# A graph-attention kernel in float32: the next group's q/k/v projections cut into quarters and laid between the attention steps of each batch

## The chip, the cores and the metric

The kernel runs on one core of a Trainium2 chip. The metric is the device time of one execution in microseconds (us), as the median of several runs. Before the change it was 3089.8 us (3 runs, 3089.11 to 3089.93). A program on one core shows no second core to compare with, so a run is called fast when it lies within 1.5% of the fastest run of the same kernel.

## The reference

The input is x of 128 batches, each 128 tokens by 512 features, with one 128x128 adjacency matrix adj. All of it is float32.

```python
# layer 0: edge convolution (both weights are adj), residual, layer norm
A = einsum('od,bdn->bon', adj, x);  C = A + b
x = layernorm(x + max over m of relu(A[m] + (C - A)[n]))
# layer 1: masked attention with 8 heads of 64, projection, layer norm, residual, layer norm
q, k, v = split(x @ w_qkv)
attn = softmax(where(adj == 0, -inf, q @ k.T * scale))
o = (attn @ v) @ w_proj + b_proj
x = layernorm(x + o + layernorm(o) * gamma + beta)
```

The largest products are the q/k/v projection (128x512 by 512x1536 for each batch) and the output projection (128x512 by 512x512). The batches do not depend on each other, which is what makes it possible to work on the projections of later batches while an earlier one is in its attention.

## The kernel before

Batches go in groups of four. `prepare(g)` does layer 0 of a group (`pa`, the normalisation, the transposes `ptx`) and then all projections of the group: eight chunks of q and k (`pq`, four matmuls each, over the 512 tokens of the group) and four of v (`pv`).

```python
def prepare(g):
    ...                                    # pa, layer norm, ptx -> xT
    for c in range(2 * KC):                # q and k: 8 chunks
        pq = ps_1.tile(...)
        for kc in range(KC):
            nc.tensor.matmul(pq, wqkv_sb[:, kc, c*P:(c+1)*P], xT[:, kc], ...)
        ...                                # q copied by ScalarE, k by VectorE, into qkT
    for i in range(G):                     # v: one chunk for each batch
        ...                                # pv, 4 matmuls; copied by ScalarE
```

`softmax` of a batch makes the scores (`psc`, eight small matmuls of 64 rows, which the trace has as 16 records, two for each float32 matmul; a transpose is one record: `ppt` has 8 for 8), adds the mask, takes the maximum, the eight exponentials, and divides. `finish` is the dependent tail, in which every TensorE step needs a copy by another engine of what the step before it made:

```python
def finish(g, i, xt, v, e):
    ...   # ppt: 8 transposes of e (TensorE) -> eT (ScalarE copy)
    ...   # pav: 8 pairs of head and value (TensorE) -> oT (ScalarE copy)
    ...   # po: output projection (TensorE) -> o, layer norms, y (VectorE, GpSimd)
```

The loop places the projections of the next group as one whole in the middle of a group:

```python
for g in range(NG):
    xt, qkT, v = ready
    for i in range(G):
        e = softmax(g, i, qkT)
        if pending is not None:
            finish(*pending)
        pending = (g, i, xt, v, e)
        if i == 1 and g + 1 < NG:
            ready = prepare(g + 1)         # 64 pq and 32 pv records in one piece
        ...
```

## Time and profile before

| | before |
|---|---|
| time, median | 3089.8 us |
| span of the profiled run | 3087.5 us |
| TensorE busy | 2555.4 us (83%) |
| TensorE idle (span less busy) | 532.1 us |
| VectorE busy | 1443.9 us (47%) |
| mean granted TensorE clock (1 is full speed) | 0.893 |
| chain that ended last, on TensorE | 60% |

The chain that ended last is the work followed back from the last instruction, at each step to what released it. The table is read in pairs. Busy 83% beside a chain that is on TensorE for only 60% says that TensorE often waits for another engine that waits for TensorE (ppt alone waits 319.2 us for VectorE). Idle time and clock belong together as well, because some of the busy time is work done at a lower clock: from 1503.17 to 1509.89 us, behind two waits, the clock is 0.54 and po takes 6.72 us, where at a clock of 1.00 it takes 3.70. The lines themselves stand in the prediction.

### The profile page before, as it was taken

How to read it: one execution, taken by the hardware profiler on the slowest of the kernel's cores; microseconds unless marked ns; L12 is line 12 of the kernel's file. 1: busy time of each engine (PE TensorE's matmuls, PEld its weight loads, DVE VectorE, ACT ScalarE, POOL GpSimd, SP SyncE). 2: the span in 40 equal slices, each digit the busy share in tenths (PEclk: the TensorE clock that was granted, in tenths of full speed). 3: DMA queues.
4: the chain of work that ended last, by engine and by line, in shares of the span. 5: the costliest groups of instructions: out<-in, count | busy, mean ns of one | idle time of the engine just before them, and what ended most of it. 6: DMA issues, size and time to landing. Idle time of an engine off the chain costs nothing.

```text
span 3087.5 us, 27231 instructions
## 1 busy us (share of the span) xinstructions
PE 2555.4 (83%) x9985; PEld 1331.7 (43%) x9985; DVE 1443.9 (47%) x2755; ACT 827.3 (27%) x2689; POOL 383.3 (12%) x422
## 2 busy tenths in 40 slices
PE   7877898777988779887798877888778987779887
PEld 3444444444444444444444444444444444444443
DVE  2355533555334553345543355433555335553346
ACT  1233222232222322223322223222232222322222
POOL 0011110111011111111110011100111101110112
PEclk9898999888998889988898888989889998889988
DMA  2000000000000000000000000000000000000000
GB/s 106 4 28 28 28 8 21 28 28 28 21 7 28 28 28 24 7 24 28 28 24 7 24 28 28 24 8 24 28 28 28 9 20 28 28 28 21 7 14 24
DMA packets 38293, 73.89 MB, mean 24 GB/s; under 512 B 2832, under 2 KB 2960, under 8 KB 38160
## 3 DMA queue, kind: packets, MB, share of 16 engines
q1 hardware_dynamic: 35328, 67.12, 6.3%
q10 hardware_dynamic: 2832, 5.05, 0.5%
q8 instruction: 78, 1.28, 0.2%
q14 instruction: 55, 0.45, 0.0%
HBM read 38.60 MB, written 33.55 MB: 23 GB/s over the span
## 4 chain that ended last, share of the span: by engine, by line
PE 60%; DVE 22%; POOL 6%; ACT 5%; issue 5%; POOLq 0%; DVEq 0%; ACTq 0%
PE pq L147 28%; PE pv L160 14%; PE po L214 11%; PE ptx L139 4%; DVE st L112 3%; POOL rstd L107 3%; ACT e L184 3%; POOL res L220 3%; DVE nmax L181 2%; DVE o L225 2%; PE pav L205 2%; DVE o L218 2%; DVE r L122 2%; DVE o L228 2%; DVE xt L127 2%
## 5 line engine op out<-in xcount | busy, mean ns | idle before, releaser
L147 PE MATMUL pq<-xT,wqkv_sb 128*128 128x512 f32 x2048 | 888.5, 594 | 1.4 <-ACT xT L140 1.3
L214 PE MATMUL po<-wproj_sb,oT 128*128 128x512 f32 x1024 | 565.1, 702 | 49.9 <-ACT oT L210 45.9
L147 PEld LDWEIGHTS pq<-xT,wqkv_sb 128*128 128x128 f32 x2048 | 389.5, 191 | 479.5 <-issue 476.7
L184 ACT ACTIVATE e<-e,nmax 128x128 f32<-128x128 f32 x1024 | 396.7, 389 | 405.8 <-DVE nmax L181 253.4
L160 PE MATMUL pv<-wqkv_sb,xT 128*128 128x512 f32 x1024 | 444.7, 592 | 0.0
L197 PE MATMUL ppt<-ident,e 128*128 128x128 f32 x1024 | 165.0, 306 | 319.2 <-DVE e L190 319.2
L154 DVE COPY qkT<-pq 128x512 f32<-128x512 f32 x128 | 88.6, 692 | 706.4 <-PE pq L147 706.4
L220 POOL TENSOR_TENSOR res<-xt,o 128x512 f32<-128x512 f32 x128 | 167.3, 1307 | 1999.5 <-DVE o L218 1994.2
L218 DVE TENSOR_TENSOR o<-po,bproj_sb 128x512 f32<-128x512 f32 x128 | 88.0, 688 | 678.8 <-PE po L214 678.7
L214 PEld LDWEIGHTS po<-wproj_sb,oT 128*128 128x128 f32 x1024 | 217.7, 224 | 312.5 <-issue 235.4
L197 PEld LDWEIGHTS ppt<-ident,e 128*128 128x128 f32 x1024 | 139.6, 161 | 383.0 <-issue 381.9
L107 POOL TENSOR_TENSOR rstd<-ve,mhalf 128x1 f32<-128x1 f32 (+1 forms) x288 | 216.7, 756 | 700.5 <-DVE ve L105 695.4
L160 PEld LDWEIGHTS pv<-wqkv_sb,xT 128*128 128x128 f32 x1024 | 194.6, 190 | 244.9 <-issue 244.9
L164 ACT COPY v<-pv 128x512 f32<-128x512 f32 x128 | 75.0, 586 | 803.6 <-PE pv L160 803.6
L205 PE MATMUL pav<-eT,v 128*64 128x128 f32 x2048 | 143.6, 284 | 89.5 <-ACT eT L199 89.2
L184 ACT ACTIVATION_READ_ACCUMULATOR e<-e,nmax 128x1 f32 x1024 | 191.8, 187 | 0.0
L140 ACT COPY xT<-ptx 128x512 f32<-128x512 f32 x128 | 74.3, 581 | 404.3 <-PE ptx L139 404.3
L205 PEld LDWEIGHTS pav<-eT,v 128*64 128x64 f32 x2048 | 111.7, 139 | 148.7 <-ACT eT L199 102.5
L179 DVE TENSOR_TENSOR e<-psc,mask 128x1024 f32<-128x1024 f32 x128 | 154.7, 1209 | 14.1 <-PE psc L174 14.1
L174 PE MATMUL psc<-qkT 64*128 64x128 f32 x2048 | 158.8, 289 | 1.1 <-ACT eT L199 1.1
L190 DVE TENSOR_TENSOR e<-e,rsum 128x1024 f32<-128x1024 f32 x128 | 156.2, 1220 | 1.2
L181 DVE TENSOR_REDUCE nmax<-e 128x8 f32<-128x1024 f32 x128 | 155.1, 1211 | 0.1
(34 smaller groups left out, 1758.8 us busy)
## 6 DMA issues: line engine op xcount, KB each, us to landing
xt<-in_x_dram SPq DMA_DIRECT2D x32, 1024.0 KB, 5.4
out_dram<-y SPq DMA_DIRECT2D x128, 256.0 KB, 2.0
wqkv_sb<-in_L_gnn_w_qkv_dram ACTq DMA_DIRECT2D x3, 1024.0 KB, 15.2
wproj_sb<-in_L_gnn_w_proj_dram ACTq DMA_DIRECT2D x1, 1024.0 KB, 18.8
bproj_sb<-in_L_gnn_b_proj_dram ACTq DMA_DIRECT2D x1, 256.0 KB, 14.4
gamma_sb<-in_L_gnn_ln_gamma_dram ACTq DMA_DIRECT2D x1, 256.0 KB, 10.5
beta_sb<-in_L_gnn_ln_beta_dram ACTq DMA_DIRECT2D x1, 256.0 KB, 10.5
adj_sb<-in_adj_dram ACTq DMA_DIRECT2D x1, 64.0 KB, 3.0
```

The lines of the kernel that those rows point to most:

```text
L107: nc.gpsimd.tensor_tensor(r, ve, mhalf[:, :n], op=ALU.pow)
L147: nc.tensor.matmul(pq, wqkv_sb[:, kc, c * P : (c + 1) * P], xT[:, kc], start=(kc == 0), stop=(kc == KC - 1),)
L160: nc.tensor.matmul(pv, xT[:, kc, i, :], wqkv_sb[:, kc, 2 * D :], start=(kc == 0), stop=(kc == KC - 1),)
L174: nc.tensor.matmul(psc[:, s, hp, :], qkT[rs, hp, i, :], qkT[rs, KC + hp, i, :], start=True, stop=True,)
L179: nc.vector.tensor_tensor(e, psc.rearrange("p s a m -> p (s a) m"), mask_b, op=ALU.add)
L181: nc.vector.tensor_reduce(nmax, e, AX.X, ALU.max, negate=True)
L184: nc.scalar.activation(e[:, j, :], e[:, j, :], AF.Exp, bias=nmax[:, j : j + 1], accum_out=sums[:, j : j + 1],)
L190: nc.vector.tensor_tensor(e, e, rsum[:, :, None].to_broadcast([P, H, P]), op=ALU.mult)
L197: nc.tensor.transpose(ppt[:, j, :], e[:, j, :], ident)
L205: nc.tensor.matmul(pav[s * HD : (s + 1) * HD, hp, :], v[:, i, h * HD : (h + 1) * HD], eT[:, s * HP + hp, :], start=True, stop=True,)
L214: nc.tensor.matmul(po, oT[:, c, :], wproj_sb[:, c, :], start=(c == 0), stop=(c == KC - 1),)
L220: nc.gpsimd.tensor_tensor(res, xt[:, i, :], o, op=ALU.add)
```

## The change

The intent is that TensorE always has something to do that waits for nothing, in each place where the attention chain would make it wait. The kernel's steps become small functions, and a loop over single batches issues them in a fixed order: between the score matmuls and `pav` lies a chunk of q, between `pav` and `po` a chunk of k, and behind `po` a chunk of v, all of the group that is needed five steps later. Layer 0 runs 9 and 14 steps ahead.

```diff
-    xpool = ctx.enter_context(tc.tile_pool(name="xpool", bufs=3))
+    xpool = ctx.enter_context(tc.tile_pool(name="xpool", bufs=7))
 ...   (prepare, softmax and finish are cut into conv, transpose_x, qk, vproj,
 ...    scores, transpose_e, attend and project, with the same instructions)
-    for g in range(NG):
-        ...
+    A_DENSE, A_TRANS, A_CONV = 5, 9, 14
+    with tc.manual_schedule(engines={mybir.EngineType.PE}):
+        for s in range(-A_CONV, B):
+            here, nxt = 0 <= s, 0 <= s + 1 < B
+            u, t, w = s + A_DENSE, s + A_TRANS, s + A_CONV
+            dense = 0 <= u < B
+            if w % G == 0 and w // G + 1 < NG:
+                load_x(w // G + 1)
+            if here:
+                eT = transpose_e(s)              # ppt
+            if nxt:
+                scores(s + 1)                    # psc of the next batch
+            if dense:
+                qk(u // G, u % G)                # pq, a chunk of q
+            if here:
+                oT = attend(s, eT)               # pav
+            if dense:
+                qk(u // G, KC + u % G)           # pq, a chunk of k
+            if here:
+                project(s, oT)                   # po
+            if dense:
+                vproj(u // G, u % G)             # pv
+            if 0 <= t < B:
+                transpose_x(t)                   # ptx
+            if w < B:
+                conv(w)                          # pa
```

The number of matmuls is the same. The four more tiles of x hold the batches that are now in flight.

More of the change, by code (lines that the diff above doesn't have):

```diff
@@ L45, in tile_adj_resnorm_d2 @@
     G = 4
+    NG = B // G
     KC = D // P
@@ L57, in tile_adj_resnorm_d2 @@
     ps_2 = ctx.enter_context(tc.tile_pool(name="ps_2", bufs=2, space=bass.MemoryType.PSUM))
+    xs, rs, qkTs, vs, xTs, es, mv0s = {}, {}, {}, {}, {}, {}, {}
     def load_x(g):
@@ L61, in load_x @@
         nc.sync.dma_start(xt, x[g * G : (g + 1) * G].rearrange("b t d -> t b d"))
-        return xt
+        xs[g] = xt
     adj_sb = const.tile([P, P], FP, name="adj_sb")
@@ L68, in tile_adj_resnorm_d2 @@
     nc.scalar.dma_start(b0_sb, b0.rearrange("(p o) -> p o", o=1))
-    x_tiles = {0: load_x(0)}
+    load_x(0)
     wqkv_sb = const.tile([P, KC, 3 * D], FP, name="wqkv_sb")
@@ L113, in stats, with conv @@
         nc.vector.bn_aggr(mv, st)
-    def prepare(g):
-        xt = x_tiles.pop(g)
-        r = small.tile([P, G], FP, tag="r", name=f"r_{g}")
-        for i in range(G):
-            pa = ps_1.tile([P, D], FP, tag="ps1", name=f"pa_{g}_{i}")
-            nc.tensor.matmul(pa, adjT, xt[:, i, :], start=True, stop=True)
-            nc.vector.tensor_reduce(r[:, i : i + 1], pa, AX.X, ALU.max)
+    def conv(b):
+        g, i = divmod(b, G)
+        xt = xs[g]
+        if i == 0:
+            rs[g] = small.tile([P, G], FP, tag="r", name=f"r_{g}")
+        pa = ps_1.tile([P, D], FP, tag="ps1", name=f"pa_{b}")
+        nc.tensor.matmul(pa, adjT, xt[:, i, :], start=True, stop=True)
+        nc.vector.tensor_reduce(rs[g][:, i : i + 1], pa, AX.X, ALU.max)
+        if i < G - 1:
+            return
+        r = rs.pop(g)
@@ L123, in prepare @@
         nc.vector.tensor_scalar(r, r, b0_sb, 0.0, op0=ALU.add, op1=ALU.max)
         mv = small.tile([P, G, 2], FP, tag="mv0", name=f"mv0_{g}")
-        for i in range(G):
-            nc.vector.tensor_scalar(xt[:, i, :], xt[:, i, :], r[:, i : i + 1], None, op0=ALU.add)
-            stats(mv[:, i, :], xt[:, i, :], f"0_{g}_{i}")
-        rstd = rstd_of(mv, G, f"0_{g}")
-        xT = group.tile([P, KC, G, P], FP, tag="xT", name=f"xT_{g}")
-        for i in range(G):
-            nc.vector.tensor_scalar(
-                xt[:, i, :], xt[:, i, :], mv[:, i, 0:1], rstd[:, i : i + 1],
-                op0=ALU.subtract, op1=ALU.mult,
-            )
-            pt = ps_1.tile([P, KC, P], FP, tag="ps1", name=f"ptx_{g}_{i}")
-            for c in range(KC):
-                nc.tensor.transpose(pt[:, c, :], xt[:, i, c * P : (c + 1) * P], ident)
-            nc.scalar.copy(xT[:, :, i, :], pt)
@@ L143, in prepare @@
-        qkT = group.tile([P, 2 * KC, G, P], FP, tag="qkT", name=f"qkT_{g}")
-        for c in range(2 * KC):
-            pq = ps_1.tile([P, G, P], FP, tag="ps1", name=f"pq_{g}_{c}")
-            for kc in range(KC):
-                nc.tensor.matmul(
-                    pq, wqkv_sb[:, kc, c * P : (c + 1) * P], xT[:, kc],
-                    start=(kc == 0), stop=(kc == KC - 1),
-                )
-            if c < KC:
-                nc.scalar.activation(qkT[:, c], pq, AF.Copy, scale=scale)
-            else:
-                nc.vector.tensor_copy(qkT[:, c], pq)
@@ L156, in prepare @@
-        v = group.tile([P, G, D], FP, tag="v", name=f"v_{g}")
-        for i in range(G):
-            pv = ps_1.tile([P, D], FP, tag="ps1", name=f"pv_{g}_{i}")
-            for kc in range(KC):
-                nc.tensor.matmul(
-                    pv, xT[:, kc, i, :], wqkv_sb[:, kc, 2 * D :],
-                    start=(kc == 0), stop=(kc == KC - 1),
-                )
-            nc.scalar.copy(v[:, i, :], pv)
-        return xt, qkT, v
-    def softmax(g, i, qkT):
-        psc = ps_2.tile([P, 2, HP, P], FP, tag="ps2", name=f"psc_{g}_{i}")
+        for j in range(G):
+            nc.vector.tensor_scalar(xt[:, j, :], xt[:, j, :], r[:, j : j + 1], None, op0=ALU.add)
+            stats(mv[:, j, :], xt[:, j, :], f"0_{g}_{j}")
@@ new lines, in conv, with transpose_x @@
+        mv0s[g] = mv, rstd_of(mv, G, f"0_{g}")
+    def transpose_x(b):
+        g, i = divmod(b, G)
+        xt = xs[g]
+        mv, rstd = mv0s[g]
+        if i == 0:
+            xTs[g] = group.tile([P, KC, G, P], FP, tag="xT", name=f"xT_{g}")
+        nc.vector.tensor_scalar(
+            xt[:, i, :], xt[:, i, :], mv[:, i, 0:1], rstd[:, i : i + 1],
+            op0=ALU.subtract, op1=ALU.mult,
+        )
+        pt = ps_1.tile([P, KC, P], FP, tag="ps1", name=f"ptx_{b}")
+        for c in range(KC):
+            nc.tensor.transpose(pt[:, c, :], xt[:, i, c * P : (c + 1) * P], ident)
+        nc.scalar.copy(xTs[g][:, :, i, :], pt)
@@ new lines, in qk @@
+    def qk(g, c):
+        xT = xTs[g]
+        if c == 0:
+            qkTs[g] = group.tile([P, 2 * KC, G, P], FP, tag="qkT", name=f"qkT_{g}")
+        pq = ps_1.tile([P, G, P], FP, tag="ps1", name=f"pq_{g}_{c}")
+        for kc in range(KC):
+            nc.tensor.matmul(
+                pq, wqkv_sb[:, kc, c * P : (c + 1) * P], xT[:, kc],
+                start=(kc == 0), stop=(kc == KC - 1),
+            )
+        if c < KC:
+            nc.scalar.activation(qkTs[g][:, c], pq, AF.Copy, scale=scale)
+        else:
+            nc.vector.tensor_copy(qkTs[g][:, c], pq)
@@ new lines, in vproj, with scores @@
+    def vproj(g, i):
+        xT = xTs[g]
+        if i == 0:
+            vs[g] = group.tile([P, G, D], FP, tag="v", name=f"v_{g}")
+        pv = ps_1.tile([P, D], FP, tag="ps1", name=f"pv_{g}_{i}")
+        for kc in range(KC):
+            nc.tensor.matmul(
+                pv, xT[:, kc, i, :], wqkv_sb[:, kc, 2 * D :],
+                start=(kc == 0), stop=(kc == KC - 1),
+            )
+        nc.scalar.copy(vs[g][:, i, :], pv)
+    def scores(b):
+        g, i = divmod(b, G)
+        qkT = qkTs[g]
+        psc = ps_2.tile([P, 2, HP, P], FP, tag="ps2", name=f"psc_{b}")
@@ L171, in softmax @@
         for hp in range(HP):
             for s in range(2):
-                rs = slice(s * HD, (s + 1) * HD)
+                hs = slice(s * HD, (s + 1) * HD)
                 nc.tensor.matmul(
-                    psc[:, s, hp, :], qkT[rs, hp, i, :], qkT[rs, KC + hp, i, :],
+                    psc[:, s, hp, :], qkT[hs, hp, i, :], qkT[hs, KC + hp, i, :],
                     start=True, stop=True,
                 )
-        e = work.tile([P, H, P], FP, tag="e", name=f"e_{g}_{i}")
+        e = work.tile([P, H, P], FP, tag="e", name=f"e_{b}")
@@ L179, in softmax @@
         nc.vector.tensor_tensor(e, psc.rearrange("p s a m -> p (s a) m"), mask_b, op=ALU.add)
-        nmax = small.tile([P, H], FP, tag="nmax", name=f"nmax_{g}_{i}")
+        nmax = small.tile([P, H], FP, tag="nmax", name=f"nmax_{b}")
         nc.vector.tensor_reduce(nmax, e, AX.X, ALU.max, negate=True)
-        sums = small.tile([P, H], FP, tag="sums", name=f"sums_{g}_{i}")
+        sums = small.tile([P, H], FP, tag="sums", name=f"sums_{b}")
         for j in range(H):
@@ L187, in softmax, with transpose_e, attend @@
             )
-        rsum = small.tile([P, H], FP, tag="rsum", name=f"rsum_{g}_{i}")
+        rsum = small.tile([P, H], FP, tag="rsum", name=f"rsum_{b}")
         nc.vector.reciprocal(rsum, sums)
         nc.vector.tensor_tensor(e, e, rsum[:, :, None].to_broadcast([P, H, P]), op=ALU.mult)
-        return e
-    def finish(g, i, xt, v, e):
-        b = g * G + i
-        ppt = ps_2.tile([P, H, P], FP, tag="ps2", name=f"ppt_{g}_{i}")
+        es[b] = e
+    def transpose_e(b):
+        e = es.pop(b)
+        ppt = ps_2.tile([P, H, P], FP, tag="ps2", name=f"ppt_{b}")
         for j in range(H):
             nc.tensor.transpose(ppt[:, j, :], e[:, j, :], ident)
-        eT = work.tile([P, H, P], FP, tag="eT", name=f"eT_{g}_{i}")
+        eT = work.tile([P, H, P], FP, tag="eT", name=f"eT_{b}")
         nc.scalar.copy(eT, ppt)
-        pav = ps_1.tile([P, HP, P], FP, tag="ps1", name=f"pav_{g}_{i}")
+        return eT
+    def attend(b, eT):
+        g, i = divmod(b, G)
+        pav = ps_1.tile([P, HP, P], FP, tag="ps1", name=f"pav_{b}")
         for hp in range(HP):
@@ L205, in finish, with project @@
                 nc.tensor.matmul(
-                    pav[s * HD : (s + 1) * HD, hp, :], v[:, i, h * HD : (h + 1) * HD],
+                    pav[s * HD : (s + 1) * HD, hp, :], vs[g][:, i, h * HD : (h + 1) * HD],
                     eT[:, s * HP + hp, :], start=True, stop=True,
                 )
-        oT = work.tile([P, HP, P], FP, tag="oT", name=f"oT_{g}_{i}")
+        oT = work.tile([P, HP, P], FP, tag="oT", name=f"oT_{b}")
         nc.scalar.copy(oT, pav)
-        po = ps_1.tile([P, D], FP, tag="ps1", name=f"po_{g}_{i}")
+        return oT
+    def project(b, oT):
+        g, i = divmod(b, G)
+        po = ps_1.tile([P, D], FP, tag="ps1", name=f"po_{b}")
         for c in range(KC):
@@ L216, in finish @@
             )
-        o = work.tile([P, D], FP, tag="o", name=f"o_{g}_{i}")
+        o = work.tile([P, D], FP, tag="o", name=f"o_{b}")
         nc.vector.tensor_tensor(o, po, bproj_sb, op=ALU.add)
-        res = work.tile([P, D], FP, tag="res", name=f"res_{g}_{i}")
-        nc.gpsimd.tensor_tensor(res, xt[:, i, :], o, op=ALU.add)
-        mv = small.tile([P, 1, 2], FP, tag="mv1", name=f"mv1_{g}_{i}")
-        stats(mv[:, 0, :], o, f"1_{g}_{i}")
-        rstd = rstd_of(mv, 1, f"1_{g}_{i}")
+        res = work.tile([P, D], FP, tag="res", name=f"res_{b}")
+        nc.gpsimd.tensor_tensor(res, xs[g][:, i, :], o, op=ALU.add)
+        mv = small.tile([P, 1, 2], FP, tag="mv1", name=f"mv1_{b}")
+        stats(mv[:, 0, :], o, f"1_{b}")
+        rstd = rstd_of(mv, 1, f"1_{b}")
         nc.vector.scalar_tensor_tensor(
@@ L228, in finish @@
         nc.vector.scalar_tensor_tensor(o, o, rstd, beta_sb, op0=ALU.mult, op1=ALU.add)
-        y = work.tile([P, D], FP, tag="y", name=f"y_{g}_{i}", bufs=4)
+        y = work.tile([P, D], FP, tag="y", name=f"y_{b}", bufs=4)
         nc.vector.tensor_tensor(y, res, o, op=ALU.add)
-        mv2 = small.tile([P, 1, 2], FP, tag="mv2", name=f"mv2_{g}_{i}")
-        stats(mv2[:, 0, :], y, f"2_{g}_{i}")
-        rstd2 = rstd_of(mv2, 1, f"2_{g}_{i}")
+        mv2 = small.tile([P, 1, 2], FP, tag="mv2", name=f"mv2_{b}")
+        stats(mv2[:, 0, :], y, f"2_{b}")
+        rstd2 = rstd_of(mv2, 1, f"2_{b}")
         nc.vector.tensor_scalar(
@@ L238, in finish @@
         nc.sync.dma_start(out[b], y)
-    NG = B // G
-    ready = prepare(0)
-    if NG > 1:
-        x_tiles[1] = load_x(1)
-    pending = None
-    for g in range(NG):
-        xt, qkT, v = ready
-        for i in range(G):
-            e = softmax(g, i, qkT)
-            if pending is not None:
-                finish(*pending)
-            pending = (g, i, xt, v, e)
-            if i == 1 and g + 1 < NG:
-                ready = prepare(g + 1)
-            if i == 2 and g + 2 < NG:
-                x_tiles[g + 2] = load_x(g + 2)
-    finish(*pending)
+    A_DENSE, A_TRANS, A_CONV = 5, 9, 14
[24 more added lines that the diff above has]
+                conv(w)
 _INS = [
```

## The prediction

> **What bounds the kernel now.** I read the page's engine shares and the chain that ended last first, then the longest waits, then one group period on TensorE in the timeline, then busy time and clock in chosen stretches of that period.
>
> ```profile
> PE 2555.4 (83%) x9985; PEld 1331.7 (43%) x9985; DVE 1443.9 (47%) x2755; ACT 827.3 (27%) x2689; POOL 383.3 (12%) x422
> ...
> PE 60%; DVE 22%; POOL 6%; ACT 5%; issue 5%; POOLq 0%; DVEq 0%; ACTq 0%
> ...
> PE ppt L197 <- DVE e L190: 319.2, 34, 10.3
> ```
>
> TensorE is busy for 83% of the span, but only 60% of the chain that set the end runs on it; VectorE and GpSimd hold 28%. No engine is saturated: the work takes turns. The third line is the largest wait of TensorE: 34 times, about once in each of the 32 groups, the transposes of the attention weights (ppt) wait some 10 us for the softmax (e).
>
> One group of four batches, TensorE only (start, length, engine, line, operation, count, in brackets the idle time before it):
>
> ```profile
> 1501.34 1.09 PE L205 MATMUL pav<-eT,v 128*64 128x128 f32 x16 [2.65 <-ACT eT L199]
> 1503.17 6.72 PE L214 MATMUL po<-wproj_sb,oT 128*128 128x512 f32 x8 [0.74 <-ACT oT L210]
> ...
> 1534.00 0.66 PE L197 MATMUL ppt<-ident,e 128*128 128x128 f32 x2 [10.32 <-DVE e L190]
> 1535.36 3.67 PE L139 MATMUL ptx<-ident,xt 128*128 128x128 f32 x16 [0.71 <-DVE xt L133]
> 1538.83 1.40 PE L197 MATMUL ppt<-ident,e 128*128 128x128 f32 x6
> 1540.06 27.63 PE L147 MATMUL pq<-xT,wqkv_sb 128*128 128x512 f32 x64
> 1567.53 13.90 PE L160 MATMUL pv<-wqkv_sb,xT 128*128 128x512 f32 x32
> 1581.36 1.09 PE L205 MATMUL pav<-eT,v 128*64 128x128 f32 x16
> ...
> 1588.60 3.70 PE L214 MATMUL po<-wproj_sb,oT 128*128 128x512 f32 x8
> 1592.14 1.04 PE L197 MATMUL ppt<-ident,e 128*128 128x128 f32 x8
> 1593.11 1.16 PE L174 MATMUL psc<-qkT 64*128 64x128 f32 x16
> 1596.92 1.09 PE L205 MATMUL pav<-eT,v 128*64 128x128 f32 x16 [2.65 <-ACT eT L199]
> ```
>
> The period is 1596.92 - 1501.34 = 95.58 us; 32 of them are 3059 us of the 3087.5. All 41 us of q/k/v projection (pq, pv) stand in one block that waits for nothing, and the attention steps, which do wait, stand bare. The same projection of the output (po, 8 records) takes 6.72 us after the waits and 3.70 us elsewhere. The stretches say why (busy time and count by engine, then granted clock, DMA share, GB/s):
>
> ```profile
> 1501.00:1510.00 9.00, 7.92 (x27) 3.76 (x28) 5.76 (x11) 4.06 (x18) 0.62 (x2) 0.62 0.08 29
> ...
> 1524.00:1534.00 10.00, 0.00 (x1) 0.04 (x1) 9.72 (x24) 0.00 (x0) 1.75 (x2) 0.62 0.07 26
> ...
> 1540.00:1567.50 27.50, 27.50 (x66) 12.23 (x65) 3.50 (x5) 5.63 (x18) 0.00 (x0) 1.00 0.00 0
> ...
> 1501.34:1596.92 95.58, 79.68 (x313) 41.48 (x313) 44.98 (x87) 25.82 (x84) 12.01 (x13) 0.89 0.06 22
> ```
>
> Two losses per period. Idle: 95.58 - 79.68 = 15.9 us. Slow clock: the cold po costs 6.72 - 3.70 = 3.0 us; the 16 ptx take 3.47 us start to start where eight warm ppt take 0.97 (1593.11 - 1592.14), so 1.5 us too many; the eight ppt of the cold stretch about 0.9. Sum 5.4. TensorE's warm work is 79.68 - 5.4 = 74.3 us per group, 18.6 us per batch against the 23.9 it gets. In 1524 to 1534 VectorE is 97% busy while TensorE has nothing: VectorE is the bound there and rests during the projections (3.50 of 27.50 us).
>
> [...] 0.62 mean clock in the two stretches above, 1.00 in the block. [...] the 64 pq records at 0.43 us each show four rotating buffers suffice here.
>
> **The change part by part.** No arithmetic is added or removed; the matmul count stays. What goes is the placement, and TensorE's order is now as written. A steady step, one batch, warm, each start to start from the timeline: ppt 0.97, psc of the next batch 1.17, pq 27.47/8 = 3.43, pav 1.02, pq 3.43, po 3.54, pv 13.83/4 = 3.46, ptx 0.97/2 = 0.49, pa two records 0.86. Sum 18.4 us, which meets the 18.6 from above; I take 18.5. The blocks are now cut up: psc to pq, pav to pq, pv to ptx, ptx to pa and pa to ppt are new switches. Eight psc before po took 0.76 us start to start where half of 1.17 is 0.585, so a switch can cost 0.18; with about half of that in four places I add 0.35. A step is 18.85 us, and 128 of them 2413 us.
>
> Does each wait fit? Step time starts at ppt. The first softmax of the trace, nearly alone:
>
> ```profile
> 68.59 1.23 DVE L179 TENSOR_TENSOR e<-psc,mask 128x1024 f32<-128x1024 f32 x1 [14.14 <-PE psc L174]
> 69.85 1.22 DVE L181 TENSOR_REDUCE nmax<-e 128x8 f32<-128x1024 f32 x1
> ...
> 74.56 1.22 DVE L190 TENSOR_TENSOR e<-e,rsum 128x1024 f32<-128x1024 f32 x1
> ...
> 75.93 1.94 PE L197 MATMUL ppt<-ident,e 128*128 128x128 f32 x8 [6.49 <-DVE e L190]
> ```
>
> From the mask add to ppt: 7.34 us. psc ends at 2.3, so e is ready at 9.6, and the next ppt comes at 18.85: 9 us to spare. eT (about 1.0 us after ppt) is ready at 2.2, pav comes at 5.8. The built order of ScalarE puts oT behind the eight exponentials and a qkT copy: 8.0 + 0.6 + 0.6 = 9.2, po comes at 10.4: 1.2 us to spare, the tightest place. VectorE then waits for po's end at 14.0; its chain to y takes 6.9 us in the trace's last batch (3077.66 to 3084.54), to 20.9, and the next psc ends at 18.85 + 2.3 = 21.15. It just fits. VectorE's work, 1443.9/128 = 11.3 us, is 60% of a step.
>
> One step in four is followed by the layer-0 burst of VectorE. The built order puts it before the next mask add. It took 4.7 us in the first group (13.15 to 17.85), so that mask add starts 4.5 us late, and four normalisations and a wait for GpSimd follow before the final multiplication of e: ready near 15.5, still before 18.85. There ScalarE's order has oT before the exponentials, so po is not held. VectorE is 1.5 us late for that step's o, and this reaches the following step's exponentials and its oT: 1.5 - 1.2 = 0.3 us of stall, 8 us in 32 groups.
>
> The ends. pq began at 24.12 us in before, after 5.5 us of warm-equivalent work, and its first block took 2.1 us more than later ones: 21 us lost. More x tiles (seven, was three) load against the weights, so I take 24. The last five steps have no projections left. There the order of VectorE (o, then e) makes a step about 10.5 us, as the last three of before (3051.78, 3061.50, 3072.09), with 6.7 us of work. Four such steps, 7.5 us to the last po and 10 us behind it are 59.5 us against 33.5 us of counted work: 26 lost.
>
> Sum: 2413 + 8 + 24 + 26 = 2471 us of span, and 2.3 us for the time over the span (3089.8 - 3087.5): 2473.
>
> **The rivals.** *Waits inside the fixed order.* If VectorE or ScalarE runs later than worked out, oT or e stops TensorE in every step. For: 1.2 us spare for oT, 0.25 us for VectorE's turn. Against: e itself has 9 us, and after mult VectorE idles until po, so delays do not add up. A stall of 1 us per step gives about 2600 us. *VectorE becomes the bound.* 60% busy speaks against it; only chain waits could do it, the case before. *Switching costs.* Every one at 0.18 us in eight places, 1.4 us per step, would make 2600; none, 2428. *The clock.* It could stay low [...]: ppt, psc and pav together last 3.2 us of a step. In 1581 to 1593 such a mix ran at 1.00, so I do not expect it; a mean of 0.95 adds some 120 us. *Transfers.* DMA is 6% busy in the period and x is loaded groups ahead: no effect in the steady state.
>
> **Range and chances.** The floor is 18.4 x 128 + 52 = about 2407 us. Stalls and switches can only add, so the range leans upwards: 2420 to 2560. For no gain of 2% the step would have to reach 23.2 us, 4.3 more than worked out; I see no chain that long. Faster 0.97, same 0.02, slower 0.01.
>
> **What would show it.** TensorE busy over 93%, mean clock at least 0.98, pq near 0.43 us per record start to start, po never near 6.7 us except in the last steps, the wait of ppt for e nearly gone, a period of four batches near 75.5 us, VectorE at 58%. Wrong would be a recurring wait of po for oT or of ppt for e above 1 us in most steps, or a clock below 0.95 in the middle.

That a wait in an engine's fixed order holds what stands behind it, which the argument takes for granted, was my assumption; e2 shows one such wait, 0.74 us before po, by which each step is longer.

## The result and the profile after

| | before | after |
|---|---|---|
| time, median of these runs | 3089.45 us (4 runs) | 2415.1 us (4 runs, 2411.12 to 2418.93) |
| span of the profiled run | 3087.5 us | 2410.0 us |
| TensorE busy | 2555.4 us | 2368.1 us |
| TensorE idle | 532.1 us | 41.9 us |
| VectorE busy | 1443.9 us | 1550.2 us |
| mean granted clock | 0.893 | 0.995 |

The ratio of after to before is 0.782, with a 95% interval of 0.7808 to 0.7833. Ratios here are the mean time of one kernel's fast runs over that of the other's of the same rounds, so they are not quite the ratio of the medians. The change is faster by more than a fifth, and 5 us beyond the fast end of the predicted range. The four runs lie in two pairs, near 2411.5 us (clock 0.995) and near 2418.7 us (0.991); so differences of a few us between kernels are read below from the steps in the traces as well as from the medians.

Of the 677.5 us that the span lost, 490 us (532.1 - 41.9) were idle time of TensorE and 187 us (2555.4 - 2368.1) were busy time for the same 9985 instructions. The engine shares and the chain that ended last, on the page of the kernel after:

```profile
PE 2368.1 (98%) x9985; PEld 1214.1 (50%) x9985; DVE 1550.2 (64%) x2755; ACT 806.2 (33%) x2689; POOL 333.5 (14%) x422
...
PE 97%; DVE 1%; DMA 0%; ACT 0%; POOL 0%; issue 0%; POOLq 0%; SPq 0%; ACTq 0%; DVEq 0%
```

TensorE is now the bound in the plain sense: busy for 98% of the span, and 97% of the chain. The two waits that matter, as total us, count and the longest in us:

```profile
PE ppt L221 <- DVE mv L122: 13.8, 4, 3.6
PE po L244 <- ACT oT L237: 3.7, 5, 0.7
```

The wait of ppt for the softmax was 319.2 us in 34 places. What is left is four waits (3.4 us in the mean), and the timeline has them all in the last steps, where no projections are left to fill in. The same holds for the five short waits of po.

One whole step on TensorE, from one ppt to the next, with the same columns as the timeline in the prediction:

```profile
1209.28 1.04 PE L221 MATMUL ppt<-ident,e 128*128 128x128 f32 x8
1210.25 1.16 PE L198 MATMUL psc<-qkT 64*128 64x128 f32 x16
1211.34 3.70 PE L168 MATMUL pq<-xT,wqkv_sb 128*128 128x512 f32 x8
1214.97 1.09 PE L232 MATMUL pav<-eT,v 128*64 128x128 f32 x16
1215.99 3.70 PE L168 MATMUL pq<-xT,wqkv_sb 128*128 128x512 f32 x8
1219.53 3.60 PE L244 MATMUL po<-wproj_sb,oT 128*128 128x512 f32 x8
1222.96 3.60 PE L183 MATMUL pv<-wqkv_sb,xT 128*128 128x512 f32 x8
1226.40 0.60 PE L157 MATMUL ptx<-ident,xt 128*128 128x128 f32 x4
1226.83 1.02 PE L132 MATMUL pa<-xt,adjT 128*128 128x512 f32 x2
1227.69 1.04 PE L221 MATMUL ppt<-ident,e 128*128 128x128 f32 x8
```

No line carries a bracket: nothing waits as long as 0.15 us, the shortest wait that is shown. The step is 1227.69 - 1209.28 = 18.41 us, and po has its warm length in a place where before it took 6.72 us. A group of four such steps, with busy time and count of PE, PEld, DVE, ACT and POOL, then granted clock, DMA share and GB/s:

```profile
1209.28:1282.94 73.66, 73.66 (x314) 37.77 (x312) 48.39 (x87) 25.13 (x84) 10.32 (x13) 1.00 0.09 29
```

TensorE is busy for all 73.66 us at full clock. The period of a group was 95.58 us, with 79.68 busy at a clock of 0.89.

What goes on beside it, in the step shown, on the other engines:

```profile
1211.53 1.22 DVE L203 TENSOR_TENSOR e<-psc,mask 128x1024 f32<-128x1024 f32 x1
...
1217.55 1.23 DVE L214 TENSOR_TENSOR e<-e,rsum 128x1024 f32<-128x1024 f32 x1
1217.67 0.57 ACT L237 COPY oT<-pav 128x512 f32<-128x512 f32 x1
```

The attention weights are ready at 1217.55 + 1.23 = 1218.78 and are not used until 1227.69, so 8.9 us are to spare. The copy oT ends at 1218.24 and po starts at 1219.53: 1.3 us to spare, the tightest place. It is tighter still by the weight load: the first load of po, which is what reads oT (in the kernel before the load waits 0.23 us for it at 1583.14), already starts at 1219.10, 0.86 us after the copy. The softmax itself takes as long as before (7.25 us from the start of the mask add at 1211.53 to 1218.78; 7.19 us before, 68.59 to 75.78); it is merely no longer waited for.

VectorE's busy time grew by 106 us with the same 2755 instructions. The mean of one record hardly moved (the multiplication by 1/sum is 1220 ns before and 1234 after). Records of instructions that follow directly on each other can overlap, by 0.08 us in the median of both traces, and busy time counts that stretch once. Added up singly, the records grew by 14 us only (1610.0 to 1624.0), while the overlap shrank by 92 us (166.1 to 73.8). So this figure is no sign of more work, and it cost nothing here.

### The profile page after: what moved, and what is told of

Its sections match the earlier page's. It is cut to its first block, busy times and chain, and to the rows that moved or that the text cites. A ratio compares the mean times of both kernels' runs of the same rounds, so it can differ in the third digit from the quotient of the medians.

```text
span 2410.0 us, 27354 instructions
## 1 busy us (share of the span) xinstructions
PE 2368.1 (98%) x9985; PEld 1214.1 (50%) x9985; DVE 1550.2 (64%) x2755; ACT 806.2 (33%) x2689; POOL 333.5 (14%) x422
## 4 chain that ended last, share of the span: by engine, by line
PE 97%; DVE 1%; DMA 0%; ACT 0%; POOL 0%; issue 0%; POOLq 0%; SPq 0%; ACTq 0%; DVEq 0%
PE pq L168 38%; PE pv L183 18%; PE po L244 18%; PE psc L198 6%; PE pav L232 5%; PE ppt L221 5%; PE pa L132 4%; PE ptx L157 2%; DMA xt<-in_x_dram 0%; DVE st L121 0%; ACT e L208 0%; DVE e L214 0%; DVE o L248 0%; POOL res L250 0%; POOL rstd L116 0%
## 5 line engine op out<-in xcount | busy, mean ns | idle before, releaser
L168 PE MATMUL pq<-xT,wqkv_sb 128*128 128x512 f32 x2048 | 945.6, 605 | 0.0
L168 PEld LDWEIGHTS pq<-xT,wqkv_sb 128*128 128x128 f32 x2048 | 368.6, 189 | 408.0 <-issue 392.1
L244 PE MATMUL po<-wproj_sb,oT 128*128 128x512 f32 x1024 | 463.1, 595 | 3.7 <-ACT oT L237 3.7
L183 PE MATMUL pv<-wqkv_sb,xT 128*128 128x512 f32 x1024 | 460.3, 592 | 0.0
L244 PEld LDWEIGHTS po<-wproj_sb,oT 128*128 128x128 f32 x1024 | 194.6, 191 | 249.6 <-issue 233.5
L116 POOL TENSOR_TENSOR rstd<-ve,mhalf 128x1 f32<-128x1 f32 (+1 forms) x288 | 175.8, 610 | 694.9 <-DVE ve L114 694.5
L213 DVE RECIPROCAL rsum<-sums 128x8 f32<-128x8 f32 x128 | 25.7, 200 | 316.1 <-ACT e L208 316.1
L223 ACT COPY eT<-ppt 128x1024 f32<-128x1024 f32 x128 | 129.6, 1012 | 149.0 <-PE ppt L221 149.0
L214 DVE TENSOR_TENSOR e<-e,rsum 128x1024 f32<-128x1024 f32 x128 | 158.0, 1234 | 4.3
L221 PEld LDWEIGHTS ppt<-ident,e 128*128 128x128 f32 x1024 | 119.4, 141 | 79.7 <-issue 65.0
L205 DVE TENSOR_REDUCE nmax<-e 128x8 f32<-128x1024 f32 x128 | 156.2, 1220 | 3.3
L221 PE MATMUL ppt<-ident,e 128*128 128x128 f32 x1024 | 133.0, 273 | 13.8 <-DVE mv L122 13.8
```

Of the source, the lines that this page charges most:

```text
L116: nc.gpsimd.tensor_tensor(r, ve, mhalf[:, :n], op=ALU.pow)
L168: nc.tensor.matmul(pq, wqkv_sb[:, kc, c * P : (c + 1) * P], xT[:, kc], start=(kc == 0), stop=(kc == KC - 1),)
L183: nc.tensor.matmul(pv, xT[:, kc, i, :], wqkv_sb[:, kc, 2 * D :], start=(kc == 0), stop=(kc == KC - 1),)
L205: nc.vector.tensor_reduce(nmax, e, AX.X, ALU.max, negate=True)
L214: nc.vector.tensor_tensor(e, e, rsum[:, :, None].to_broadcast([P, H, P]), op=ALU.mult)
L221: nc.tensor.transpose(ppt[:, j, :], e[:, j, :], ident)
```

## The experiments

My theory was that the gain is the waits and the low clock behind them, both removed by the independent work that now lies in the chain. Three questions were to be told apart: what a switch between kinds of matmul costs, since the step was shorter than predicted; whether each pair of dependent steps needs its own quarter of filler, or one place in the step is enough; and whether the gain comes from the spreading of the projections or from the early scores. The theories in each run's expectation are rivals on these questions. Eight kernels were run, all with right results, in two sets, each set on one chip with its own runs of the kernel before (median 3089.18 us of 9 runs for e5, e4, e2 and e6; 3086.93 us of 7 runs for e8, e9, e3 and e7). Ratios are to those runs. Diffs are against the changed kernel.

**e1, built and not run: the directive taken away.**

```diff
-    with tc.manual_schedule(engines={mybir.EngineType.PE}):
+    if True:
```

The built program has the same instructions, in the same order and with the same waits, on all five engines. So the directive by itself changes nothing here; the order in which the loop issues the work does. Nothing was left to run.

**e5: more switches.** The first chunk of pq and pav are interleaved, one pq matmul and then the pav of two heads, four times. TensorE does the same matmuls and returns from small to full ones three more times in each step.

```diff
-            if dense:
+            if here and dense:
+                oT = attend_qk(s, eT, u // G, u % G)   # for hp in range(4): 1 pq matmul, 2 pav matmuls
+            elif dense:
                 qk(u // G, u % G)
-            if here:
+            elif here:
                 oT = attend(s, eT)
```

> Each step's first q/k quarter is interleaved matmul by matmul with the eight attention-times-v matmuls: q, 2 pav, q, 2 pav and so on, where the changed kernel has 4 q then 8 pav. Same work; three more switches from small tiles back to a full-array matmul per step, and three more the other way. Theory A (double counting: only a switch from psc or pav to a full-array matmul costs, 0.11 to 0.20 us as in the changed kernel's trace, and my prediction had counted the new ones without crediting the old ones): a step of 18.75 to 19.0 us, 42 to 77 us more than the changed kernel, near 2457 to 2492 us. Theory B (the prediction's term: about 0.09 us on any switch): six more switches, 0.53 us a step, about 2483 us. Theory C (switches are free): 2415 us. A and B are told apart by where the time goes between starts in the trace, A and C by the total.

Measured: 2545.06 us (5 runs, 2539.26 to 2545.38), ratio 0.8234 [0.8223, 0.8245], outside every range that I had given. The step, on TensorE:

```profile
1214.78 1.04 PE L221 MATMUL ppt<-ident,e 128*128 128x128 f32 x8
...
1216.84 1.12 PE L248 MATMUL pq<-xT,wqkv_sb 128*128 128x512 f32 x2
1217.90 0.44 PE L254 MATMUL pav<-eT,v 128*64 128x128 f32 x4
1218.27 1.12 PE L248 MATMUL pq<-xT,wqkv_sb 128*128 128x512 f32 x2
...
1234.24 1.04 PE L221 MATMUL ppt<-ident,e 128*128 128x128 f32 x8
```

The step is 1234.24 - 1214.78 = 19.46 us against 18.41: 1.05 us for three more round trips, 0.35 us each, with no wait anywhere and a mean clock of 0.992. Start to start, a pq pair takes 1.06 us where two records among full ones take 3.43/4 = 0.858: 0.20 us more. The pq pair has small ones on both sides, so each side of a full run costs some 0.1 us. Four pav records take 0.37 us and sixteen 1.02, so a record is (1.02 - 0.37)/12 = 0.054 us, and each run of pav costs another 0.15 us once, an estimate from these two lengths that takes this share as the same in both. Together that is the 0.35. Over the 123 steps that have both pieces, 1.05 us makes 129 us, which is the difference in time (2545.06 - 2415.1 = 130). So a switch between the full 128x128 matmuls and those of 64 columns for one head is real. A round trip is two switches, so one costs 0.175 us, which is the 0.18 that I had read from the profile before; but that was luck, since most of what I had read there was a wait, as told below. What the switch does inside TensorE, this run does not tell.

**e4: pav directly behind psc.** The first chunk of q moves behind pav, so the pair of small groups stands together. One return to full matmuls less, and no filler between ppt and pav but psc.

```diff
-            if dense:
-                qk(u // G, u % G)
             if here:
                 oT = attend(s, eT)
+            if dense:
+                qk(u // G, u % G)
```

> The attention-times-v matmuls (pav) move from behind the first q/k quarter to directly behind the scores, so no projection lies between ppt and pav. Theory A (only small-to-full switches cost; psc hides the copy of eT): one such switch less, 0.11 to 0.20 us, against a wait of up to 0.1 us for eT: 0 to 0.1 us less per step, 2402 to 2415 us. Rival (a quarter must lie between each pair of dependent steps): pav waits for eT by 1 us per step, about 2540 us.

Measured: 2406.53 us (2401.78 to 2407.76), ratio 0.7788 [0.7778, 0.7799]. The step is 18.35 us (1224.59 - 1206.24).

```profile
1207.20 1.16 PE L198 MATMUL psc<-qkT 64*128 64x128 f32 x16
1208.43 1.09 PE L232 MATMUL pav<-eT,v 128*64 128x128 f32 x16
1209.45 7.13 PE L168 MATMUL pq<-xT,wqkv_sb 128*128 128x512 f32 x16
```

Here psc to pav is 1.22 us start to start where psc to pq was 1.09. The weight loads of pav now wait for eT in 125 steps, 0.25 us each. The step lost only 0.06 us (0.08 in the mean of 108 steps), which in 128 steps is 8 to 10 us, as the time shows (2415.1 - 2406.53 = 8.6). So the return that was taken away is worth less than 0.35 us in this place: the two chunks of pq, now one run, take 6.98 us where they took 3.63 + 3.54 = 7.17, but psc to pav became 0.13 us longer. Whether that is the wait for eT or a switch from 64 rows to 64 columns, this run does not tell. It does tell that a quarter of the projections between each two dependent steps is not needed: psc alone covers the copy eT but for those 0.25 us.

**e2: all filler in one place in the step.** ppt, psc, pav and po stand together, and then both chunks of pq, pv, ptx and pa.

```diff
-            if dense:
-                qk(u // G, u % G)
             if here:
                 oT = attend(s, eT)
-            if dense:
-                qk(u // G, KC + u % G)
             if here:
                 project(s, oT)
+            if dense:
+                qk(u // G, u % G)
+            if dense:
+                qk(u // G, KC + u % G)
```

> Same pipeline one batch ahead, but in each step the four attention steps stand together (ppt, psc, pav, po) and the three projection quarters behind them. Theory: the long wait (e, 7.3 us) stays covered by the quarters, only the short waits come back: po for oT as in the kernel before (1.83 us from pav's start to po's where pav alone takes 1.02, so 0.8 us) and up to 0.1 us for eT: a step of 19.2 to 19.4 us, 2515 to 2540 us, clock still above 0.98. Rival 1 (the quarters between the steps are what matters): over 2700. Rival 2 (only the quarter per batch matters, the place within the step does not): 2415 us.

Measured: 2507.44 us (2506.98 to 2508.09), ratio 0.8118 [0.8107, 0.8129], clock 0.993.

```profile
1222.32 3.70 PE L244 MATMUL po<-wproj_sb,oT 128*128 128x512 f32 x8 [0.74 <-ACT oT L237]
```

The one wait that comes back is that of po for oT, 0.74 us in each step. The step is 19.16 us, and (19.16 - 18.41) x 128 = 96 us is nearly the difference in time (2507.44 - 2415.1 = 92). It is the expected mechanism, 8 us below the expected range. The filler between pav and po is thus worth 0.74 us a step, and po stays at its warm 3.70 us behind such a short wait. Most of the gain is there already with filler in one place in each step.

**e3: the projections of a group in one block again.** Everything else stays as in the changed kernel, the softmax one batch ahead too.

```diff
-            if dense:
-                qk(u // G, u % G)
 ...
-            if dense:
-                qk(u // G, KC + u % G)
 ...
-            if dense:
-                vproj(u // G, u % G)
+            if dense and u % G == 0:
+                for c in range(2 * KC):
+                    qk(u // G, c)
+                for i in range(G):
+                    vproj(u // G, i)
```

> The same pipeline and lookahead, attention one batch ahead, but the twelve projection pieces of a group stand in one block in every fourth step; the other three steps are bare. Theory: bare steps are paced by VectorE and ScalarE as the last steps of the changed kernel are (11.2 to 12.5 us), the block step takes some 49 us, a period 83 to 87 us: 2700 to 2850 us, with a granted clock well below 0.98. Rival (the pipelining one batch ahead is what counts, not the spreading): below 2500 us.

Measured: 2988.28 us (2987.79 to 2989.75), ratio 0.9683 [0.9667, 0.9699], some 140 us beyond the slow end of what I expected. The clock is 0.939, TensorE busy 2487.2 us. The three bare steps of a group each end in a wait, which is that of the next ppt:

```profile
1326.86 1.06 PE L221 MATMUL ppt<-ident,e 128*128 128x128 f32 x8 [2.06 <-DVE mv L122]
...
1338.30 1.06 PE L221 MATMUL ppt<-ident,e 128*128 128x128 f32 x8 [2.44 <-DVE ve L114]
...
1356.14 1.94 PE L221 MATMUL ppt<-ident,e 128*128 128x128 f32 x8 [7.31 <-DVE e L214]
```

The period before these lines is 92.35 us (1315.78 - 1223.43): three bare steps of 11.1, 11.4 and 18.1 us, and one step of 51.7 us with the block. What I had not charged is the burst of layer 0 on VectorE, which by the order of the program falls into a bare step. In the changed kernel it makes e ready 14.25 us into the step instead of 9.5; here ppt waits 7.31 us for e. In the changed kernel the same burst has a full step of filler over it. The kernel before had its softmax one batch ahead as well, so the early scores cannot be what is new. Breaking up layer 0 and fixing the order, with the block left whole, brings 99 us against the runs of its own set (3086.93 - 2988.28); spreading the block brings 573 us more (2988.28 - 2415.1), which is 85% of the gain of 674 us (3089.45 - 2415.1). Experiments e2 and e3 together say what kind of spreading it is: one place in every step is nearly enough, one place in every fourth step is not.

**e7: the scores issued last in the step.** The other way round: the filler stays spread, but psc of the next batch stands behind po and leaves the softmax only pv, ptx and pa to hide under.

```diff
-            if nxt:
-                scores(s + 1)
 ...
             if here:
                 project(s, oT)
+            if nxt:
+                scores(s + 1)
```

> Every step as in the changed kernel, but the scores of the next batch come behind the projection po, so only pv, ptx and pa (4.7 us) lie between psc and the next ppt instead of 16 us. Theory: ppt waits for e, which needs 7.3 us from psc alone and more here, as VectorE's work on o of the same step stands in its way (about 10.9 us from po's end to e, against 6.0 us of TensorE work): 4.9 us idle per step, more in every fourth, 3000 to 3300 us, near the kernel before or slower. Rival (the cover of the softmax is ample in either place): 2415 us.

Measured: 3382.36 us (3381.85 to 3384.83), ratio 1.096 [1.0943, 1.0976], slower than the kernel before, and 82 us beyond the slow end of what I expected (3300).

```profile
1249.35 1.94 PE L221 MATMUL ppt<-ident,e 128*128 128x128 f32 x8 [4.80 <-DVE e L214]
1251.08 5.61 PE L168 MATMUL pq<-xT,wqkv_sb 128*128 128x512 f32 x8
```

The wait of 4.80 us is nearly what I had worked out (4.9). What I had left out is the clock, 0.888 in the mean of this run against 0.995: behind that wait ppt takes 1.94 us for 1.04, and the next pq 5.61 us for 3.70. That step is 25.09 us (1249.35 - 1224.26), one of the shorter ones: in the mean of 108 steps it is 25.9 us, 7.5 more than in the changed kernel, of which the wait is 5.3 (676.1 us in 128 places). So spread filler alone is not what wins: without the early scores it loses to the kernel before.

**e6: v projected late.** The v chunk of a batch is made one step before it is used, so that the last steps still have projections as filler.

```diff
-    A_DENSE, A_TRANS, A_CONV = 5, 9, 14
+    A_DENSE, A_TRANS, A_CONV, A_V = 5, 9, 14, 1
 ...
-            if dense:
-                vproj(u // G, u % G)
+            if 0 <= s + A_V < B:
+                vproj((s + A_V) // G, (s + A_V) % G)
```

> The v projection of a batch is made one step before it is used, not five, so four of the five bare last steps get 3.43 us of v projection each. Steady state unchanged. Theory: the last steps are paced by VectorE and ScalarE (11.2 to 12.5 us per step against 6.7 us of TensorE work), so the added 3.43 us is hidden in them: 4 x 3.43 = 13.7 us less, 2401 us. Rival (the projections only push the chain of the last steps along, since ppt stands behind pv): no gain, 2415 us.

Measured: 2654.64 us (2653.07 to 2659.04), ratio 0.8597 [0.8585, 0.8608], a miss: it lost 240 us to the changed kernel. The wait that tells it:

```profile
ACT xT L158 <- PE pv L183: 319.1, 30, 14.2
```

The transposed x of a group, xT, has two buffers. The first ptx of a group is copied into its buffer 9 steps before its first batch, and the last pv now reads it 2 steps behind that, in the group's own time: 11 steps of life, where two buffers allow 8. With v at five steps ahead the last read is just in time. Once in each group the copy waits for pv, 10.4 us in nearly all of the 30 places (the last number of the line is the longest). TensorE stops too, for copies of ScalarE and for VectorE: in the period from 1207.47 to 1289.38 pq waits 1.75 us for qkT and 0.74 for oT, pav 0.69 for qkT, po 2.04 for VectorE's qkT, and with three shorter ones (pa 0.24, pv 0.78, ptx 0.68) it is 6.92 us. The period is 81.91 us against 73.66. By which way the late copy of xT leads to each of these waits, the trace does not show; that it is the buffer, e8 does.

**e8: e6 with a third buffer for xT.** This tests that reading. The edit is that of e6 and this line.

```diff
-            xTs[g] = group.tile([P, KC, G, P], FP, tag="xT", name=f"xT_{g}")
+            xTs[g] = group.tile([P, KC, G, P], FP, tag="xT", name=f"xT_{g}", bufs=3)
```

> The late v projection again, with three buffers for xT where the failed run had two. Theory: the 240 us of that run came from a buffer: v of group g reads xT of group g until four steps later than before, while the transposes of group g + 2 already want to write the same buffer, and their copies stop ScalarE and with it TensorE; with a third buffer the step is 18.41 us again and the gain at the end remains: 2400 to 2408 us. Rival (the late v projection itself, or the ScalarE order it leads to, is what cost): about 2650 us.

Measured: 2399.81 us (2397.24 to 2402.09), ratio 0.7775 [0.7763, 0.7786]. The buffer was the whole cause of e6's loss. And what e6 was made for now comes: the last steps take no longer with pv in them (11.3 to 12.4 us), because ppt now waits 0.2 to 1.2 us where it waited 3.4. The pv that they took over is missing at the start, where the first ppt comes at 75.5 us instead of 85.97. The kernel is 15 us faster than the changed one by the medians, 10 us by the profiled runs.

**e9: e8 and e4 together.**

> Both edits together: pav directly behind the scores (0.06 us less per step in the trace of that run, 8 us in all), and the late v projection with three xT buffers (up to 13.7 us less at the end). Theory: the gains add, 2393 to 2400 us. If the last steps are the longer for pv, 2407 us.

The edit is the three diffs of e4, e6 and e8. Measured: 2388.69 us (2388.36 to 2389.1), ratio 0.7739 [0.7727, 0.775], clock 0.997. The gains of e4 (8.6 us) and e8 (15.3 us) add up to 23.9 of the 26.4 us that it gains, 4 us below the expected range. It beats both kernels, and lies 1.1% under the changed one.

## Why the prediction was wrong by its number and right by its chain

The prediction was 2473 us with a range of 2420 to 2560; the kernel took 2415.1. The span was predicted as 2471 us and was 2410.0: 61 us to explain.

*The step, which failed.* The term of the sum that was mis-sized is "I take 18.5" for a sum of 18.4, and then "with about half of that in four places I add 0.35". The step measured 18.41 us. (18.85 - 18.41) x 128 = 56 us of the 61. Piece by piece, start to start:

| piece | predicted | measured |
|---|---|---|
| ppt | 0.97 | 0.97 |
| psc | 1.17 | 1.09 |
| pq, first | 3.43 | 3.63 |
| pav | 1.02 | 1.02 |
| pq, second | 3.43 | 3.54 |
| po | 3.54 | 3.43 |
| pv | 3.46 | 3.44 |
| ptx | 0.49 | 0.43 |
| pa | 0.86 | 0.86 |
| sum | 18.37, then 18.85 | 18.41 |

The step that failed is the addition itself: I added the cost of new switches to old durations from which I had not taken the cost of their old neighbours. The two are nearly equal, and that is chance. First, switches do cost, but only where TensorE goes between full matmuls and those of 64 rows or columns for one head: 0.20 us with the first pq, which has such ones on both sides, and 0.11 us with the second, which has them only in front, 0.31 together. The switches among full ones (pv to ptx, ptx to pa, pa to ppt), which I had charged too, cost nothing that the table shows. The share that a run of small matmuls bears itself (0.15 us for pav, by e5) stood in the old 1.02 already. Second, the durations that I took from the kernel before were too long by 0.27 us for their new places: po stood behind psc there and stands behind a full pq now (0.11), the 1.17 for psc is what the timeline before has where pav follows it (1510.70 to 1511.87), and pq follows it now (0.08), the pv block ended at pav (0.02), and I had taken ptx from ppt, which is followed by psc (0.06). So 0.31 was to be added and 0.27 to be taken off; I added 0.35 and a rounding of 0.13 and took nothing off. Experiment e5 shows what a round trip costs when it is really added: 0.35 us.

The evidence for the 0.18 us was misread in part as well. In the kernel before, the eight psc in front of po lasted 0.76 us until po in part because po waited for its input:

```profile
1582.38 0.72 PE L174 MATMUL psc<-qkT 64*128 64x128 f32 x8
1582.50 0.59 ACT L210 COPY oT<-pav 128x512 f32<-128x512 f32 x1 [0.45 <-PE pav L205]
1583.14 0.30 PEld L214 LDWEIGHTS po<-wproj_sb,oT 128*128 128x128 f32 x2 [0.23 <-ACT oT L210]
```

The copy oT ends at 1583.09 and the weights of po load at 1583.14. From the start of the last psc record to that of the first po record it is 0.31 us here and 0.35 in the median of the 61 such places, and 0.20 us to pq in the changed kernel, where nothing waits. So 0.11 to 0.15 of the 0.18 us were a wait, too short to be shown as one on TensorE, and I took it for the cost of a switch. The real cost stood in the same stretch: this po, with psc in front and pav behind, took 3.63 us start to start (1586.77 - 1583.14), the next one, with psc in front and ppt behind, 3.54 us, and a po between full matmuls takes 3.43 us after the change.

*The waits inside the order, right.* I worked out e as ready 9.6 us into the step and 9 us to spare; measured are 9.5 and 8.9. For oT I had 9.2 us and 1.2 to spare, measured 8.96 and 1.3.

*The layer-0 burst, too dear.* In a step that has it, I had e ready at 15.5 us and the o of that step 1.5 us late, with 8 us of stall in 32 groups. Measured are 14.25 us and 0.3 us, and no stall at all.

*The ends, nearly right.* 24 us at the start and 26 us in the last steps were 50 us; the span less 128 steps of 18.41 leaves 2410.0 - 2356.5 = 53.5. The last steps took 11.2 to 12.6 us where I had about 10.5: ppt waits 3.4 us for VectorE, and in two of them psc then runs slow (2.08 us for 1.16; clock 0.64 from 2353.34 to 2358.10 and 0.68 from 2377.00 to 2382.40). Together the terms make up the difference: 56 + 8 - 3.5 = 60.5 us. (The excess of the first block at the start, 2.1 us in the prediction, is 1.96 us start to start in the trace before: 53.55 - 24.12 - 27.47. It changes nothing.)

*The signs to watch.* TensorE above 93% (98%), clock at least 0.98 (0.995), no cold po in the middle, and the wait of ppt gone: all as written. The period of four batches was predicted as 75.5 us and was 73.66. VectorE was predicted at 58% and shows 64%; the union of its records grew by 106 us, as told above, where I had left it as it was.

*The range.* Its low end of 2420 us was above my own floor of 2407, and the kernel ran at 2415.1. I wrote that stalls and switches "can only add" to the floor and leaned the range upwards for it. But the floor's own 18.4 held as much of the old switches and neighbours (0.27 us) as the new ones were to cost (0.31), so a result near the floor was the likely one.

*The rivals.* None of them came. The clock stayed at 1.00 through the steps, VectorE did not become the bound, and no wait for oT recurred. Experiment e2 shows what the first of them would have been: 0.74 us a step, 92 us. Experiment e7 shows what a real loss looks like: a wait of 5.3 us in the mean of its 128 steps, and the clock with it (0.888).

## What to carry to other kernels

When a chain of dependent steps alternates with independent work, spread the independent work so that each step has some of it, and issue the start of the chain as early as the buffers allow: here the spreading is worth 573 us of the 674, and it only pays with the early scores (without them, e7, 3382.36 us). Before lengthening the life of a tile, count the steps from its first write to its last read against its buffers; one buffer too few cost 240 us here. In a sum of durations taken from a profile, look at what each was adjacent to, because the cost of a switch, or a wait, can be in them already; what is added for new neighbours has to be set against what the old ones cost.

## What the runs show of the switches, the clock and the buffers

- Switches: a round trip from full matmuls to the 64-column ones of pav and back costs 0.35 us (1.05 us for three, e5), while switches among the full shapes cost nothing that the table of pieces shows. No run shows what in TensorE takes the time.
- Clock: in the kernel before, po took 6.72 us for 3.70 at a clock of 0.54 (1503.17 to 1509.89), behind idle times of 2.65 and 0.74 us with 1.09 us of pav between them. In e7, behind one gap of 4.80 us, the next pq took 5.61 us for 3.70 (mean clock of the run 0.888). In e2, with a gap of 0.74 us in each step, the clock was 1.00 from 1000 to 2000 us (0.993 in the mean of the run). The length of one gap does not decide in these traces: behind 2.44 us in e3 psc takes 1.93 us for 1.16, and behind 3.35 us at the end of the changed kernel it takes 1.16, at a clock of 1.00 (2365.87 to 2369.00). What does decide, no run here shows.
- Transposes: in the changed kernel eight transposes (ppt) in each step, in 0.97 us, go with a clock of 1.00 (1209.28 to 1282.94), in the middle of other work; no run has them alone.
- Buffers: the late v with two buffers of xT takes 2654.64 us (e6) and with three 2399.81 us (e8).
